# A two-layer decoder kernel: five edits to its mask products, its head norms, its query transposes, its second convolution and its down products

## The chip, the cores and the metric

The kernel runs on one core of one Trainium2 chip. A core has a matrix engine (PE, TensorE; its weight loads are listed as PEld), a vector engine (DVE, VectorE), an activation engine (ACT, ScalarE), a general-purpose engine (POOL, GpSimd) and a queue that issues DMAs (SP, SyncE). PE writes its products to PSUM, which is cut into banks of 128 partitions x 512 float32 values; the other tiles lie in SBUF. Each engine works through its own list of instructions in order and waits at an instruction until what it needs is there.

The metric is the device time of one execution in microseconds (us), and the median over runs is what counts. The time is lower for a better kernel.

## The reference, cut to what matters

The input is `x` (4 sequences, 256 positions, 256 channels) and a context of the same 4 x 256 positions with 128 channels. Two layers follow each other. Each has self-attention, a state-space block that reads the context, and a feed-forward block, each added to `x`.

```
x += L0_attn(layernorm(x))          # 8 query heads of 32, 2 key heads, window of 64 positions
x += L0_mamba(ctx, layernorm(x))
x += L0_ffn(layernorm(x))           # silu(x Wg) * (x Wu), 704 wide, then the down product
x += L1_attn(layernorm(x))          # 16 query heads of 128, 4 key heads, causal
x += L1_mamba(ctx, layernorm(x))
x += L1_moe(layernorm(x))           # 32 experts of 128, weighted by a router, and a shared one
```

In the first attention each head of q, k and v is made zero-mean and divided by its root mean square, and the scores go through a soft cap: `tanh(s / 30) * 30`. Positions outside the window are masked before it.

The state-space block, the same in both layers but for its weights, is

```
xin = ctx @ in_proj.T                         # 256 channels
u   = silu(causal_conv(xin, 4 taps) + bias)   # each channel by itself
dt, Bm, Cm = split(u @ x_proj.T);  dt = softplus(dt @ dt_proj.T + b)
h[t] = h[t-1] * exp(dt[t] * A) + dt[t] * u[t] * Bm[t]     # 16 states per channel
y[t] = sum over states of h[t] * Cm[t];  out = (y + D u) * silu(z)
```

In the second attention the norm of each query head of 128 is followed by a rotation. The norm's root only scales the scores, so it is applied to them and not to the queries.

## The kernel before, in words

Everything is float32 but the mask product. Tokens lie on the partitions in 8 tiles of 128, two per sequence. Time runs in four stages, which overlap at their borders because an engine's list is filled with what is ready.

**The first stage** (`stage_a`, to about 206 us) holds the first attention for the four sequences and most of the first layer's scan. `head0(b)` normalizes a sequence, projects it (L356), rotates it, and takes the head norms: a reduce (L380), the subtraction of the mean (L381), squares (L385), a reduce (L388), and then `rsqrt_steps` (L100 to L112) on 24 columns: one integer guess and three rounds of four short DVE operations, 13 instructions. The result scales the queries (L396), the values (L399) and, on POOL, the keys (L403). `tail0(b)` transposes queries and keys (L424, L429) and computes the scores of two heads at a time in two PSUM banks. The mask is added by a product: `identb` times `far` puts 0 or a large negative number into each bank, and the score products (L453, 32 rows of the array) are added to it. The loop at L447 issues this mask product three times per bank. The first two are overwritten by the third, since each starts its bank anew. Then follow tanh (L462), exp (L470), the products with the values (L476 to L487, 33 columns each), the division (L412, L413), a transpose (L497), and the output product (L506).

Between these, the generator `states` runs the scan: for one state and one half of the channels, ACT takes an exp (L215), POOL multiplies (L217), DVE scans (L218) and multiplies (L220), and the result is added either by a PE product with the identity (L235) or by POOL (L237). The rows for it come by DMA, two per state (L209), issued by SP. The tiles of this chain have three buffers, and the exp's PSUM tile has two.

**The front of the state-space block**, `mamba_front(l, bp, pool)`, serves two sequences `bp` of layer `l`. Input projection and convolution are one step: `conv_taps(l)` (L297) builds on DVE and PE four weight matrices, one per tap (L304, L311, L312). For each half of the channels four products with shifted context (L166) then add up in one bank, and ACT applies bias and silu out of the bank (L173). `conv_taps(1)` is called at L590. The fronts of layer 1 are called at L639, at the end of each half of the feed-forward block, but their convolutions depend on nothing but the context and are done much earlier. The bank is that of the pool `pf`, which has one.

**The feed-forward stage** (to about 310 us) works in two halves of 512 tokens: gates and layer norm, then for each of six blocks of 128 hidden channels the gate and up products (L606), silu (L614) and their product on DVE (L617). Each half ends with the down products: for two token pairs `t2` a bank is taken from the pool `pa`, which has one bank, 12 products are added up in it (L630), and DVE adds the bank to `x` (L638). The pool `pc`, also of one bank, serves gates and layer norms here.

**The second attention** (to about 651 us) walks over 4 sequences x 4 key heads, 16 steps. A step works on three things at once: `queries` of this step, `score` of the step before, `finish` of the one before that. `queries(xnT, g, qT)` (L710) does for both token tiles `c`: `rotate`, a projection into one of two banks (L673), four squares with sums on ACT (L688), and three DVE operations (L693, L700, L701) that leave the rotated queries in `qr`, which has two buffers; then `transposed`, four PE transposes (L707) into one of two banks of the pool `ps_t`, and an ACT copy (L708) into `qT`. At the end comes the root of the norm on POOL (L666). `score` computes the products of one key head (L771, then L780 twice, through one bank of `ps_s` until step 12), which DVE scales and masks (L773, L789), the maxima (L794, L795), the exps (L799) and on POOL the division (L804). `finish` transposes the weights and multiplies them with the values (L814 to L835), and every second step the output product follows (L842). The scan of the second layer runs beside this, 19 of its 32 double steps in the first 13 steps.

**The expert stage** (to the end) is a train of products (L974, L988).

What sets the order: the program's order gives each instruction its rank, but a planner draws up each engine's list when the kernel is built. It plays the program through with estimated durations, and where the next instruction in rank isn't ready it takes a later one that is. So a step of the scan often stands between two steps of a head norm. An instruction that the planner thought ready, and that isn't, holds all that stands behind it on its engine.

Of the kernel before, what the change touches and what calls it, by code (L numbers as in the profile page):

```python
# [41 lines left out]
def decoder_kernel(  # L42
# [34 lines left out]
    def ps(pool):  # L77
        return pool.tile([P, 512], F32, tag="ps", name="ps")
# [71 lines left out]
    def mamba_front(l, bp, pool):  # L150
# [11 lines left out]

        for c in range(2):
            pi = ps(pool)
            for k in range(4):
                mm(  # L166
                    pi.rearrange("p (b t) -> p b t", b=2),
                    lhsT=taps[:, k, c * P : (c + 1) * P],
                    rhs=ctxT[:, 2 * bp : 2 * bp + 2, k : k + S],
                    start=(k == 0),  # L170
                    stop=(k == 3),
                )
            nc.scalar.activation(  # L173
                u[:, c, :], pi, AF.Silu, bias=par[:, o + M_CONVB + c : o + M_CONVB + c + 1]
            )
# [143 lines left out]
    with ExitStack() as ph:  # L319
# [27 lines left out]
        def head0(b):  # L347
# [39 lines left out]
            rs24 = rs.rearrange("p c h -> p (c h)")  # L387
            nc.vector.tensor_reduce(rs24, sq, AX.X, ALU.add)  # L388
            nc.vector.tensor_scalar(rs24, rs24, 1.0 / 32, 1e-6, ALU.mult, ALU.add)
            rs = rsqrt_steps(rs24, 24).rearrange("p (c h) -> p c h", c=2)  # L390
            qn = ap.tile([P, 2, 8, 32], F32, tag="qn", name="qn")
            krep = ap.tile([P, 2, 2, 4, 32], F32, tag="krep", name="krep")

# [25 lines left out]
        def tail0(b, qn, krep, vn, states):  # L419
# [20 lines left out]
            for g in range(2):  # L440
                pr = prs[g]

                for jp in range(2):
                    psc = [ps(pb) for _ in range(2)]


                    for last in range(3):  # L447
                        for p_ in psc:
                            mm(p_[:, 0:320], lhsT=identb, rhs=far, start=True, stop=(last < 2))
                    for klo, qlo, lo, hi in ((0, 0, 0, NEAR), (P, P, NEAR, 320)):  # L450
                        for p_, j in zip(psc, (2 * jp, 2 * jp + 1)):
                            hp = slice(32 * j, 32 * j + 32)
                            mm(  # L453
                                p_[:, lo:hi],
                                lhsT=qkT[hp, 2 + g, klo : klo + P],
                                rhs=qkT[hp, g, qlo : qlo + hi - lo],
                                start=False,
                                stop=(klo > 0),
                            )
                    for p_, j in zip(psc, (2 * jp, 2 * jp + 1)):  # L460
                        for lo, hi in ((0, NEAR), (256, 384)):
                            nc.scalar.activation(  # L462
                                pr[:, j, lo:hi],
                                p_[:, lo and NEAR : (lo and NEAR) + hi - lo],
                                AF.Tanh,
                                scale=256.0 / (math.sqrt(32.0) * SOFTCAP),
                            )
# [109 lines left out]
    with ExitStack() as ph:  # L577
# [9 lines left out]
        nc.sync.dma_start(out=dw, in_=down_in)  # L587
        nc.gpsimd.tensor_mul(dw, dw, downs.unsqueeze(1).to_broadcast([P, NIC, HID]))

        conv_taps(1)  # L590
        scans = []
        for hf in range(2):
            szs = [gates_of(2 * hf + bb, fp, 4) for bb in range(2)]
# [29 lines left out]
                    ALU.mult,  # L623
                )
            for t2 in range(2):
                pd = ps(pa)
                for t in range(2):
                    for ic in range(NIC):
                        m = min(P, INTER - ic * P)
# [14 lines left out]
    with ExitStack() as ph:  # L644
# [62 lines left out]
                nc.tensor.transpose(pt[:, i * P : (i + 1) * P], qr[:, i, :], ident)  # L707
            nc.scalar.copy(dst[:, :, c * P : (c + 1) * P], pt.rearrange("p (h t) -> p h t", h=4))  # L708

        def queries(xnT, g, qT):  # L710

            ss = small.tile([P, 2, 4], F32, tag="qss", name="qss")
            for c in range(2):
                transposed(rotate(xnT, c, g, ss[:, c, :]), c, qT)
            return rsqrt(ss, qks)

        def keys_values(b):
            xnT = work.tile([P, 2, S], F32, tag="xnT", name="xnT")
# [320 lines left out]
        for b in range(B):  # L1039
            xnT, kT = keys_values(b)  # L1040
            for g in range(NKV1):
                qT = ap.tile([P, 4, S], F32, tag="qT", name="qT", bufs=2)
                rq = queries(xnT, g, qT)
                queued.append((b, g, qT, rq, kT, xnT))
                if len(queued) > 1:
                    score()
                if len(scored) > 1:
                    finish()
                step = 4 * b + g
# [137 lines left out]
```

## Time and profile before

| | |
|---|---|
| runs before | 898.40, 910.52 and 914.03 us; median 910.52 |
| the profiled execution | 899.79 us, of which 898.0 us are the span from first to last instruction |
| granted PE clock over the span | 0.947 of full |
| PE busy | 806.3 us, 3074 products |
| DVE busy | 588.0 us |
| ACT busy | 474.5 us |
| POOL busy | 423.5 us |
| chain that ended last | PE 51%, DVE 20%, ACT 10%, issue 5%, POOL 4% |

How to read it: the busy time of an engine is the sum over its instructions. PE's records overlap, so that a stretch of full PE can hold reserves. In the profile, rows cut in slices show how busy an engine was in each part of the span, and the row of the granted clock says at which share of its full speed PE ran. A group of instructions is named by its line in the kernel; after its busy time and mean duration stands how long its engine was idle just before it, and for what. The chain of waits follows the work that ended last back to what released it. Times "from 56 to 206" count from the span's start.

### The profile page before, as it was taken

The page shows a single profiled execution, that of the slowest core. Times are in us where ns is not written, and L with a number is a line of the kernel's source. Part 1 is how long each engine was busy: PE and PEld are TensorE (multiplying, and loading weights), DVE is VectorE, ACT ScalarE, POOL GpSimd, SP SyncE. Part 2 cuts the span into 40 slices and gives each one's busy share as a digit, 9 for nine tenths or more (in the row PEclk, how much of TensorE's full clock was granted, in tenths as well). Part 3 has the DMA queues.
Part 4 walks back from the last instruction along what each step waited for, and adds up shares of the span by engine and source line. Part 5 has one row for each costly group of instructions (what it writes and reads, how often), then busy time and mean ns, then how long its engine had stood idle before and what let it go on. Part 6 is the DMA issues. An engine that isn't in the chain of part 4 may idle for free.

```text
span 898.0 us, 10284 instructions
## 1 busy us (share of the span) xinstructions
PE 806.3 (90%) x3074; PEld 501.4 (56%) x3074; DVE 588.0 (65%) x1106; ACT 474.5 (53%) x1182; POOL 423.5 (47%) x427
## 2 busy tenths in 40 slices
PE   4888999978989887889788978997999999999997
PEld 1445656523444444647555755665666656666665
DVE  4799988985855588797769686787057676212121
ACT  2767544587949556657857754776333433211111
POOL 5456676976645527766547471422257751000000
PEclk9999767978998999999899989997999999999999
DMA  5347564583512401101112010000147753445442
GB/s 162 117 133 252 174 187 157 186 275 100 198 64 68 143 1 36 59 33 39 36 36 72 23 47 1 24 3 24 27 152 226 231 152 104 148 149 162 156 144 82
DMA packets 60999, 98.36 MB, mean 110 GB/s; under 512 B 6336, under 2 KB 26704, under 8 KB 60688
## 3 DMA queue, kind: packets, MB, share of 16 engines
q1 hardware_dynamic: 59232, 95.77, 33.6%
q10 hardware_dynamic: 1712, 1.94, 0.7%
q8 instruction: 24, 0.39, 0.2%
q14 instruction: 31, 0.25, 0.1%
HBM read 96.24 MB, written 1.44 MB: 109 GB/s over the span
## 4 chain that ended last, share of the span: by engine, by line
PE 51%; DVE 20%; ACT 10%; issue 5%; POOL 4%; DMA 1%; DVEq 0%; POOLq 0%; SPq 0%; ACTq 0%
PE ps L974 13%; PE ps L988 12%; PE ps L842 5%; DVE h L218 4%; PE ps L673 3%; DVE hc L220 2%; PE ps L606 2%; PE ps L630 2%; PE ps L827 2%; DVE ps L700 2%; ACT sc L799 2%; DVE qs L693 2%; PE ps L780 1%; ACT L215 1%; PE ps L235 1%
## 5 line engine op out<-in xcount | busy, mean ns | idle before, releaser
L217 POOL TENSOR_TENSOR db<-bt,du 128x512 f32<-128x512 f32 x128 | 162.4, 1280 | 90.7 <-DVE h L218 76.3
L218 DVE TENSOR_TENSOR_SCAN h<-h,db 128x512 f32<-128x512 f32 x128 | 152.9, 1217 | 25.9 <-ACT h L215 25.7
L974 PE MATMUL ps<-moe_xnT,w 128*128 128x512 f32 x272 | 129.0, 597 | 0.0
L988 PE MATMUL ps<-w,hT 128*128 128x256 f32 x544 | 128.7, 380 | 0.0
L979 DVE SCALAR_TENSOR_TENSOR hT<-ps,gr 128x512 f32<-128x512 f32 x64 | 44.1, 689 | 127.0 <-PE ps L974 127.0
L988 PEld LDWEIGHTS ps<-w,hT 128*128 128x128 f32 x544 | 103.2, 191 | 40.2 <-issue 29.4
L215 ACT ACTIVATE h<-dt,negA 128x512 f32<-128x512 f32 x128 | 86.2, 689 | 56.3 <-DVE hc L220 55.7
L980 ACT ACTIVATE hT<-hT 128x512 f32<-128x512 f32 x68 | 42.8, 629 | 133.8 <-DVE hT L979 133.6
L673 PE MATMUL ps<-wqkv,xnT 128*128 128x512 f32 x192 | 93.2, 597 | 8.0 <-DVE rq L665 5.6
L220 DVE TENSOR_TENSOR hc<-h,ct 128x512 f32<-128x512 f32 x128 | 85.1, 680 | 4.0 <-DMA ct<-bc 2.5
L227 POOL TENSOR_TENSOR y<-y,hc 128x512 f32<-128x512 f32 x64 | 80.8, 1274 | 7.1 <-DVE hc L220 7.1
L666 POOL TENSOR_TENSOR rq<-rq,nhalf 128x8 f32<-128x8 f32 x20 | 33.0, 1648 | 88.2 <-DVE rq L665 88.0
L974 PEld LDWEIGHTS ps<-moe_xnT,w 128*128 128x128 f32 x272 | 51.7, 191 | 36.5 <-issue 33.2
L688 ACT ACTIVATE sq<-ps 128x128 f32<-128x128 f32 x160 | 42.4, 282 | 46.2 <-PE ps L673 46.2
L799 ACT ACTIVATE sc<-sc,nm 128x256 f32<-128x256 f32 (+1 forms) x128 | 56.7, 449 | 12.2 <-DVE nm L794 8.0
L804 POOL TENSOR_TENSOR sc<-sc,rsum 128x512 f32<-128x512 f32 (+1 forms) x32 | 46.3, 1468 | 35.2 <-DVE rsum L802 33.6
L842 PE MATMUL ps<-wo,oT 128*128 128x256 f32 x256 | 57.0, 381 | 0.4 <-ACT oT L835 0.4
L842 PEld LDWEIGHTS ps<-wo,oT 128*128 128x128 f32 x256 | 48.1, 190 | 9.2 <-ACT oT L835 2.6
L673 PEld LDWEIGHTS ps<-wqkv,xnT 128*128 128x128 f32 x192 | 32.9, 190 | 29.1 <-issue 17.9
L235 PE MATMUL ps<-hc,ident 128*128 128x512 f32 x64 | 40.6, 723 | 8.1 <-DVE hc L220 8.1
L707 PE MATMUL ps<-ident,qr 128*128 128x128 f32 x160 | 28.7, 297 | 19.2 <-DVE qr L701 17.3
L237 POOL TENSOR_TENSOR y<-y,hc 128x512 f32<-128x512 f32 x32 | 40.8, 1275 | 10.4 <-DVE hc L220 5.3
(201 smaller groups left out, 1447.3 us busy)
## 6 DMA issues: line engine op xcount, KB each, us to landing
bt<-bc SPq DMA_DIRECT2D x96, 256.0 KB, 3.6
ct<-bc SPq DMA_DIRECT2D x96, 256.0 KB, 3.7
w<-in_w_dram SPq DMA_DIRECT2D x64, 256.0 KB, 3.4
gr<-gt SPq DMA_DIRECT2D x64, 256.0 KB, 3.5
wqkv<-in_wqkv_dram SPq DMA_DIRECT2D x1, 3072.0 KB, 14.4
wo<-in_wo_dram SPq DMA_DIRECT2D x1, 2048.0 KB, 8.9
x<-in_x_dram SPq DMA_DIRECT2D x4, 256.0 KB, 5.6
w<-in_ws_dram SPq DMA_DIRECT2D x4, 256.0 KB, 3.4
```

Source lines behind the costliest of these rows:

```text
L215: nc.scalar.activation(h, dt[:, c, :], AF.Exp, scale=negA[:, a : a + 1])
L217: nc.gpsimd.tensor_mul(db, bt, du[:, c, :])
L218: nc.vector.tensor_tensor_scan(h, h, db, 0.0, ALU.mult, ALU.add)
L220: nc.vector.tensor_mul(hc, h, ct)
L227: nc.gpsimd.tensor_add(y[:, c, :], y[:, c, :], state(n, c, bt, ct))
L235: mm(yp, lhsT=ident, rhs=hc, start=(n == 0), stop=(n == 14))
L673: mm(pq, lhsT=xnT[:, f, c * P : (c + 1) * P], rhs=wqkv1[:, f, ch * 512 : (ch + 1) * 512], start=(f == 0), stop=(f == 1),)
L799: nc.scalar.activation(part, part, AF.Exp, bias=nm[:, qc, j : j + 1], accum_out=rsum[:, qc, j : j + 1])
L804: nc.gpsimd.tensor_mul(part, part, rsum[:, qc, :].unsqueeze(2).to_broadcast([P, 4, w]))
L842: mm(pout[:, c * 256 : (c + 1) * 256], lhsT=oTs[h // 4][:, h % 4, c * P : (c + 1) * P], rhs=wo1[:, 8 * gp + h, :], start=(h == 0), stop=(h ...
L974: mm(ph_, lhsT=w[:, f * P : (f + 1) * P], rhs=xnT[:, f, :], start=(f == 0), stop=(f == 1))
L988: mm(po[t // 2][:, (t % 2) * 256 : (t % 2 + 1) * 256], lhsT=h[:, t * P : (t + 1) * P], rhs=w[:, 256:512], start=start and t % 2 == 0, stop ...
```

## The change

1. The mask product of a score bank is issued once, where it was issued three times. There are 32 banks in all, so 64 products of 128 x 320 fall away.
2. The root of the head norms, 24 columns in each of four `head0` calls, is one POOL instruction (a power of -0.5) instead of 13 DVE instructions. The router's `rsqrt_steps` (L945) stays.
3. In a step of the second attention, `queries` now ends after both rotations and the root. The score of the step before comes next, and only then the eight transposes and two copies. `qT` is taken after the score.
4. Layer 1's convolution is done by DVE. One product with the plain projection fills the bank, without shifts, and one DVE multiplication and three multiply-adds on shifted pieces of it give the convolution in SBUF, to which ACT applies bias and silu. `conv_taps(1)` falls away.
5. The two down products of a half take their banks from `pa` and `pc` in turn.

```diff
         for c in range(2):
             pi = ps(pool)
+            if l == 1:
+
+                mm(
+                    pi.rearrange("p (b t) -> p b t", b=2),
+                    lhsT=taps[:, c * P : (c + 1) * P],
+                    rhs=ctxT[:, 2 * bp : 2 * bp + 2, 3 : S + 3],
+                    start=True,
+                    stop=True,
+                )
+                w = par[:, o + M_CONVW + 4 * c : o + M_CONVW + 4 * c + 4]
+                uc = u[:, c, :].rearrange("p (b t) -> p b t", b=2)
+                pt = pi.rearrange("p (b t) -> p b t", b=2)
+                nc.vector.tensor_scalar(uc, pt, w[:, 3:4], None, ALU.mult)
+                for k in range(1, 4):
+                    nc.vector.scalar_tensor_tensor(
+                        uc[:, :, k:S], pt[:, :, 0 : S - k], w[:, 3 - k : 4 - k], uc[:, :, k:S], ALU.mult, ALU.add
+                    )
+                nc.scalar.activation(
+                    u[:, c, :], u[:, c, :], AF.Silu, bias=par[:, o + M_CONVB + c : o + M_CONVB + c + 1]
+                )
+                continue
             for k in range(4):
...
-            rs = rsqrt_steps(rs24, 24).rearrange("p (c h) -> p c h", c=2)
+            nc.gpsimd.tensor_tensor(rs24, rs24, nhalf, ALU.pow)
...
-                    for last in range(3):
-                        for p_ in psc:
-                            mm(p_[:, 0:320], lhsT=identb, rhs=far, start=True, stop=(last < 2))
+                    for p_ in psc:
+                        mm(p_[:, 0:320], lhsT=identb, rhs=far, start=True, stop=False)
...
-        conv_taps(1)
...
-                pd = ps(pa)
+                pd = ps((pa, pc)[t2])
...
-        def queries(xnT, g, qT):
+        def queries(xnT, g):
 
             ss = small.tile([P, 2, 4], F32, tag="qss", name="qss")
-            for c in range(2):
-                transposed(rotate(xnT, c, g, ss[:, c, :]), c, qT)
-            return rsqrt(ss, qks)
+            qrs = [rotate(xnT, c, g, ss[:, c, :]) for c in range(2)]
+            return qrs, rsqrt(ss, qks)
...
+                qrs, rq = queries(xnT, g)
+                if queued:
+                    score()
                 qT = ap.tile([P, 4, S], F32, tag="qT", name="qT", bufs=2)
-                rq = queries(xnT, g, qT)
+                for c in range(2):
+                    transposed(qrs[c], c, qT)
                 queued.append((b, g, qT, rq, kT, xnT))
-                if len(queued) > 1:
-                    score()
```

## The prediction

> **What bounds the kernel now.** I read the page's rows by slice first, then the busy time by stage, then the first stage window by window, then groups, waits and time line where an edit falls.
>
> ```profile
> PE   4888999978989887889788978997999999999997
> DVE  4799988985855588797769686787057676212121
> PEclk9999767978998999999899989997999999999999
> ```
>
> The rows say that PE is the fullest engine everywhere, and that the clock it is granted dips in the first quarter and a little later. By stage (us, then busy time with count of PE, PEld, DVE, ACT, POOL, then clock):
>
> ```profile
> 56.00:206.00 150.00, 136.04 (x585) 81.62 (x584) 130.97 (x202) 87.19 (x165) 107.48 (x100) 0.82 0.61 197
> 206.00:310.00 104.00, 92.03 (x257) 44.06 (x255) 64.95 (x107) 76.82 (x93) 60.20 (x73) 0.95 0.36 117
> 310.00:651.00 341.00, 300.74 (x1265) 199.39 (x1266) 251.60 (x524) 215.89 (x770) 166.31 (x140) 0.96 0.09 30
> 651.00:898.00 247.00, 239.87 (x853) 158.62 (x851) 102.86 (x195) 65.56 (x104) 59.94 (x57) 0.99 0.50 155
> ```
>
> The last stage is a train of products that no edit touches: 247 us stay. The first stage is held by PE and DVE in turn, and the clock decides whose turn it is. Same columns, short windows:
>
> ```profile
> 111.00:114.40 3.40, 3.40 (x29) 2.89 (x28) 3.40 (x8) 1.02 (x2) 2.74 (x4) 1.00 0.19 67
> 121.20:124.60 3.40, 2.73 (x9) 1.32 (x8) 3.40 (x6) 2.35 (x7) 3.38 (x4) 0.50 0.53 127
> 131.40:134.80 3.40, 3.40 (x9) 2.52 (x8) 0.70 (x2) 0.00 (x0) 0.38 (x1) 0.52 0.71 239
> 145.00:148.40 3.40, 3.40 (x10) 1.60 (x8) 3.28 (x5) 1.53 (x3) 3.36 (x4) 0.50 0.51 161
> 158.60:162.00 3.40, 3.40 (x23) 2.02 (x21) 3.40 (x5) 2.67 (x7) 3.40 (x4) 1.00 0.47 154
> ```
>
> At full clock DVE is full. At 0.5 PE takes over, at worst with DVE down to 0.70 of 3.40. Dips follow stretches of small products (29 in one window), about 10 us after each rise: up at 63, down at 74; up at 77, down at 91; up at 94, down at 104; up at 111, down at 121; up at 135, down at 145. From 155 to 192, where sixteen convolution products (L166) run, it stays up.
>
> **Mask products.** 64 of 96 fall away.
>
> ```profile
> L235 PE MATMUL ps<-hc,ident 128*128 128x512 f32 x46 | 31.3, 768 | 8.1 <-DVE hc L220 8.1
> L449 PE MATMUL ps<-far,identb 128*128 128x320 bf16 x79 | 16.8, 349 | 2.9 <-ACT pr L462 2.7
> L166 PE MATMUL ps<-ctxT,taps 128*128 128x512 f32 x26 | 14.6, 678 | 0.5 <-DVE taps L312 0.5
> ```
>
> On the chain from 24 to 190 L449 has 4.0%, 6.6 us; two thirds are 4.4 us gained. Against that stands the clock. The Trainium skill, "TensorE: Matmul & The Clock Gate", section "Why this matters for your kernels", would have the clock fall only after PE-idle gaps of about 3 us. PE's longest wait from 56 to 206 is 2.1 us, so by the rule nothing cools and the edit is worth -4.4. The trace disagrees: the clock is 0.5 in windows where PE records 3.40 of 3.40, so density counts, and these products are the densest work among the scores. Between 121 and 155 seven half-clock windows leave DVE 18.3 of 23.8 us busy: 0.8 us lost in each. Of the 39 windows between 56 and 190 twelve are at half now. If twelve more are, that is 10 us, less 4.4: +6. Bounds: -5 if the clock doesn't care. For the other end I add up PE's need there at the full-clock paces of the chain: 46 L235 at 0.43 are 19.8, 79 L449 at 0.135 are 10.7, 112 L453 at 0.10 are 11.2, 26 L166 at 0.43 are 11.2, 192 value products at 0.11 are 21.1, all others 27: 101 us. The edits take 7.1 (53 mask products), 8.4 (three quarters of L166) and 1.7 (L311). At half clock throughout, 63 doubles to 126, the value products take 0.137 each (26), and PE's waits stay (13.8): 166 against 150, so +17.
>
> **Head norms' root.** Two rows with the same instruction on POOL, 8 and 2 columns:
>
> ```profile
> L666 POOL TENSOR_TENSOR rq<-rq,nhalf 128x8 f32<-128x8 f32 x20 | 33.0, 1648 | 88.2 <-DVE rq L665 88.0
> L126 POOL TENSOR_TENSOR ln_rs<-ln_rs,nhalf 128x2 f32<-128x2 f32 x6 | 4.3, 714 | 0.5
> ```
>
> (1648 - 714) / 6 is 156 ns per column; 24 columns are 714 + 22 x 156 = 4.1 us, an estimate from these rows. "GPSIMD Engine Reference", section "Elementwise — side-by-side cycle accounting", has 2.6 cycles per element for a two-input operation; that would make the root some 0.5 us, 2 us for four, against 16.6 by the rows. The rows are for a power, so I take them. DVE loses 52 short instructions, 19.6 us in the trace (3.3 + 5.4 + 2.1 + 5.4 + 3.4 on L104 and L108 to L111; undisturbed, as at 30.3 to 33.1, 2.8 us per head). What is queued behind: DVE's L396 and L399, with the scan steps the planner put after them, wait for the root; L666's reader L726 waited 3.4 us in all for four such roots, half their length. Half of 4.1 plus half a POOL operation in front (0.6) is 2.7 us per head, 11 us. On POOL, 67% to 75% busy there, four times 4.1 us stand ahead of L217, and DVE's scans wait for that; three buffers of `db` cover two of them, 2.6 us, leaving 1.5 x 4 = 6. So 11 + 6 - 16 (what of 19.6 isn't overlapped records) is about +1, and the first head, uncovered, takes 4.1 for 2.8: +2 in all. Bounds: -12 (all waits covered) to +10 (no cover: 19 + 6 - 16 + 1).
>
> **Query transposes.** Per step eight L707, two copies L708 and two turns of `ps_t` move behind 8 + 8 recorded products of the score, eight scalings on DVE, the exps on ACT and two POOL multiplications. No DMA moves. PE stood 17.3 us for L701 ahead of L707, 14.3 of it in four stalls. One of them:
>
> ```profile
> 438.90 1.12 PE L707 MATMUL ps<-ident,qr 128*128 128x128 f32 x4 [3.21 <-DVE qr L701]
> 440.87 2.08 PE L780 MATMUL ps<-kT,qT 128*128 128x256 f32 x4 [0.85 <-DVE sc L773]
> ```
>
> The product behind the transposes waits for DVE as well, and so it does at 358 (0.46) and 525 (1.31). With the transposes out of the way PE stands as long for L773 and does the transposes later. Only the stall at 611 (4.72) has nothing of the kind: gain 0 to 5. The cost: the two `qr` buffers are freed later, behind products that wait for DVE between banks (0.48 to 1.2 us each), so the next step's L701, and with it the projection banks, may wait. If half a us per step isn't covered, 16 steps cost 8; the cover is that the next L701 comes a projection and three DVE operations later. I take +2, bounds -6 and +12.
>
> **Layer-1 convolution.** Each of four halves: six recorded products fewer, 2.6 us of PE; four DVE operations from PSUM more. The nearest row is L979 (689 ns, same form and size): 2.76 us, 11 us in all. Gone are L304 (1.63), two L312 (1.37) and L311. At 171 to 185 DVE is full: two halves cost 5.5 there, less 3.0: +2.5. The other two (203 to 208 and 256 to 259) find DVE 62% busy and PE on the chain at half clock: -2 to +1. In front of silu 3.44 us become 0.86 + 2.76. The table loads around silu (1.28 us each, 8% of that stage's chain) may fall elsewhere: 2 either way. Together +3, bounds -4 and +8. The lost heat of L166 at 171 to 185 is in the clock sum above.
>
> **Down products.** L638 (0.69) and its signals stand between the two L630 groups in each half: at 303.1 on the chain, 0.65; at 248.8 hidden behind L235. Ten products more can also slip under the silu's table loads. -2, bounds -4 and 0; `pc` is wanted by the second half's gates, which have other work behind them.
>
> **Sum.** 6 + 2 + 2 + 3 - 2 = +11 us: 899.8 becomes 911 for an execution like the profiled one. This lies 10.7 below the median of the runs, so the median of 910.5 becomes 922.
>
> **The rivals.** *Small costs* (52%): the sum above, 908 to 938; 33 of the 52 below the bound of 2% (928.7), which is about what a measurement of this kernel can tell.
>
> *Relief* (20%): DVE is the true bound of the first stage (131 of 150), the clock doesn't react, and DVE gets its 16 us with waits covered. -5 - 8 + 0 + 2 - 2 = -13: 897. For it: full DVE in every full-clock window. Against it: row DMAs (L209) ended waits of 4.8 and 5.6 us on the chain and don't get faster.
>
> *Cold stage* (23%), slower: without the dense products and L166 the clock stays at half from 56 to 206. Need is 63 / c + 24 + 14 us at a clock of c; PE decides from c below 0.56, and at 0.5 the stage costs +17. With +2, +2, +3 and the second half's share the sum is about +24: 934, up to 950. For it: the dips ten us after each rise. Against it: dense work (L235, L506) has always brought it back within 14 us.
>
> *It doesn't happen* (5%): the planner fills the same gaps with the same transposes and only the mask and root edits show: 912.
>
> **Numbers.** Faster: half of relief, 0.11. Slower: the cold stage and 19 of small costs, 0.42. Same: 0.47. The range 889 to 947 leaves out a tenth on each side.
>
> **What would show it.** Clock from 56 to 206 at 0.65 to 0.75; POOL roots of 4.1 us with idle DVE at L396; waits at L707 gone and waits at L780 longer; DVE 8 us fuller around 171 to 260. I am wrong if the clock rises, if roots are short, or if the second attention moves by over 10 us through its order alone.

## The result, and the profile after

| | before | after |
|---|---|---|
| median of runs | 906.38 us (898.40 to 914.03) | 926.34 us (925.70 to 935.24) |
| ratio | | 1.0257, interval [1.0208, 1.0307] |
| profiled span | 898.0 us | 923.9 us |
| last addition to `x` of the feed-forward stage begins | 309.8 us | 333.0 us |
| last addition to `x` of the second attention begins | 651.2 us | 678.1 us |

The changed kernel is slower by 2.6%. The forecast of 922 us lies 4 us from the median, but it was counted from 910.5 us, the median of three runs of the kernel before, and with the fourth run that median is 906.4: forecast was a rise of 11 us, and measured is one of 20 us (medians) to 23 us (ratio). The profiled executions differ by 26 us. Of these, 23 are there at the end of the feed-forward stage, 4 more come in the second attention (341.4 us long before, 345.1 after), and the expert stage gives 1 back. So the first two stages decide.

The rows by slice of the changed kernel, to be held against those of the kernel before:

```profile
PE   4878889965986979889978988996999998999997
DVE  3467877686685759879868974867337676312221
PEclk9888877566995999999999999998999999999999
```

A slice is 23.1 us. From 115 to 231 us the clock has five slices in a row at 7, 7, 5, 6 and 6, and one more at 5 from 277 to 300. The kernel before had 7, 6 and 7 from 90 to 157, one 7 from 180 to 202, and none below 8 in the feed-forward stage after that. The stages of the changed kernel in numbers (us, busy time with count of PE, PEld, DVE, ACT, POOL, then clock, DMA share and GB/s):

```profile
56.00:206.00 150.00, 127.09 (x499) 79.23 (x498) 112.67 (x162) 80.50 (x156) 108.15 (x92) 0.73 0.53 176
206.00:310.00 104.00, 80.67 (x188) 34.35 (x189) 70.16 (x113) 69.59 (x88) 56.62 (x71) 0.78 0.40 120
310.00:651.00 341.00, 299.19 (x1226) 192.03 (x1224) 261.91 (x537) 218.27 (x756) 174.36 (x150) 0.97 0.12 38
651.00:898.00 247.00, 242.41 (x892) 162.55 (x892) 104.29 (x197) 75.25 (x132) 67.59 (x63) 1.00 0.49 150
```

From 56 to 206 the clock went from 0.82 to 0.73, and from 206 to 310 from 0.95 to 0.78. The counts and busy times of PE and DVE are lower too, but the edits themselves took away most of that (the mask products, and of DVE's 19.6 us of steps for the root the 13.8 that came after 56 us). How far the stage had come is better read from the scans: 45 had been begun by 206 us, where the kernel before had begun 49. The third and fourth stage run at 0.97 and 1.00.

Short windows of the changed kernel, 3.4 us each, same columns:

```profile
168.20:171.60 3.40, 3.40 (x16) 3.11 (x15) 0.00 (x0) 1.11 (x3) 3.40 (x4) 0.50 0.52 156
171.60:175.00 3.40, 3.40 (x14) 2.76 (x13) 1.56 (x3) 0.84 (x3) 0.71 (x1) 0.50 0.25 74
175.00:178.40 3.40, 3.40 (x10) 1.53 (x9) 3.36 (x7) 0.24 (x1) 2.98 (x3) 0.50 0.34 118
181.80:185.20 3.40, 3.40 (x18) 3.40 (x18) 1.39 (x2) 0.75 (x2) 3.09 (x7) 0.50 0.59 199
```

The same four windows of the kernel before:

```profile
168.20:171.60 3.40, 2.76 (x16) 1.95 (x15) 2.65 (x4) 2.63 (x7) 3.40 (x4) 1.00 0.66 217
171.60:175.00 3.40, 3.40 (x19) 2.42 (x19) 3.40 (x5) 1.38 (x2) 2.89 (x3) 1.00 0.84 260
175.00:178.40 3.40, 3.40 (x10) 1.44 (x9) 3.40 (x7) 1.10 (x2) 3.17 (x4) 1.00 0.69 255
181.80:185.20 3.40, 3.40 (x11) 1.69 (x9) 2.98 (x4) 3.36 (x6) 3.09 (x6) 1.00 0.84 242
```

In this stretch (171 to 184 us) the kernel before ran 16 of the 32 recorded convolution products of layer 1, at full clock. Now PE is recorded as full and granted one half, and in the first window DVE has nothing to do at all.

The clock is not all of it. From 24 us to the end of the feed-forward stage PE was busy for 254.4 us and idle for 31.4 in the kernel before, and busy for 257.0 and idle for 52.0 in the changed one. So PE, with some hundred products fewer on record, is busy 3 us longer, at a lower clock; the other 21 us are waits of PE, and the lists further down say for what.

The groups of the edits in the changed kernel:

```profile
L256 PE MATMUL ps<-hc,ident 128*128 128x512 f32 x64 | 49.2, 869 | 20.9 <-DVE hc L241 19.4 <-DVE y L260 1.4
...
L724 PE MATMUL ps<-ident,qr 128*128 128x128 f32 x160 | 28.3, 301 | 18.2 <-DVE qr L718 15.0 <-DVE qr L742 2.4
...
L467 PE MATMUL ps<-far,identb 128*128 128x320 bf16 x32 | 9.8, 354 | 2.4 <-ACT qkT L455 1.7 <-ACT pr L480 0.7
...
L167 PE MATMUL ps<-ctxT,inproj 128*128 128x512 f32 x8 | 5.3, 755 | 2.1 <-DVE u L179 1.7 <-ACT dt L211 0.4
```

L467 is the mask product (L449 before), now 32 of it and 9.8 us, for 96 and 19.6 us. L167 is the projection and what is left of the convolution products (L166 before), L256 the addition to the scan's sum (L235 before), L724 the query transposes (L707 before).

The waits by reason, from the list of the changed kernel for all of PE and, in the second fence, for DVE from 0 to 215 us (engine, line, what it waited for: us in total, times, longest):

```profile
PE ps L256 <- DVE hc L241: 19.4, 10, 4.2
PE ps L724 <- DVE qr L718: 15.0, 11, 4.7
PE ps L796 <- DVE sc L789: 2.9, 3, 1.7
```

```profile
DVE qn L417 <- POOL a_rs L411: 16.3, 4, 4.8
DVE rr L387 <- PE ps L377: 13.2, 6, 4.6
```

The additions to the scan's sum now wait 19.4 us for DVE, 8.1 before. The scalings of the heads (L417, before L396) wait 16.3 us for the new root, more than DVE waits for any other thing in this stretch. The transposes wait 15.0 us for the rotated queries, 17.3 before: moving them behind the scores did not take this wait away. A stall of 3.92 us, in the time line of the changed kernel's PE (start, us, line, operation, tiles, and the idle time before it):

```profile
461.74 0.61 PE L787 MATMUL ps<-kT,qT 128*128 128x128 f32 x4
462.18 0.60 PE L724 MATMUL ps<-ident,qr 128*128 128x128 f32 x4
466.70 1.09 PE L724 MATMUL ps<-ident,qr 128*128 128x128 f32 x4 [3.92 <-DVE qr L718]
467.58 0.64 PE L830 MATMUL ps<-ident,sc 128*128 128x128 f32 x2
468.01 1.88 PE L796 MATMUL ps<-kT,qT 128*128 128x256 f32 x4
```

In the program all score products (L787 and L796) now precede the transposes. The planner has put both halves of the transposes (L724) behind L787 and still ahead of L796: L787 of the next step comes only at 472.96. PE waits for the second half's queries, and the score products stand behind it.

### The profile page after: what moved, and what is told of

The parts are those of the page before. It is cut to its first block, busy times and chain, and to the rows that moved or that the text cites. A ratio compares the mean times of both kernels' runs of the same rounds, so it can differ in the third digit from the quotient of the medians.

```text
span 923.9 us, 10063 instructions
## 1 busy us (share of the span) xinstructions
PE 808.6 (88%) x2982; PEld 499.5 (54%) x2982; DVE 580.4 (63%) x1067; ACT 473.9 (51%) x1182; POOL 438.9 (48%) x431
## 4 chain that ended last, share of the span: by engine, by line
PE 41%; DVE 13%; ACT 5%; issue 2%; POOL 2%; DMA 0%; SPq 0%; ACTq 0%; DVEq 0%; POOLq 0%
PE ps L1004 12%; PE ps L990 12%; PE ps L858 5%; PE ps L690 3%; ACT sc L815 2%; DVE h L239 2%; PE ps L796 2%; PE ps L843 2%; DVE qs L710 1%; PE ps L724 1%; DVE ps L717 1%; DVE qr L718 1%; ACT sq L705 1%; DVE sc L805 1%; POOL rq L683 1%
## 5 line engine op out<-in xcount | busy, mean ns | idle before, releaser
L256 PE MATMUL ps<-hc,ident 128*128 128x512 f32 x64 | 49.2, 869 | 20.9 <-DVE hc L241 19.4
L724 PE MATMUL ps<-ident,qr 128*128 128x128 f32 x160 | 28.3, 301 | 18.2 <-DVE qr L718 15.0
```

Source lines behind the costliest of these rows:

```text
L256: mm(yp, lhsT=ident, rhs=hc, start=(n == 0), stop=(n == 14))
```

## The experiments

Three theories stood against each other. *Clock*: what falls away is dense work, TensorE is granted half its speed more often, and the loss follows the granted clock. *Order*: every edit makes the planner draw up other lists, and the new lists are worse. *Work*: the instructions that the edits add (four DVE operations per convolution half, the root on POOL) cost what is lost.

Where a ratio is given, it is against runs of the kernel before on the same chip. "Clock, all runs" is the granted clock over a whole execution, as the median of the runs that the ratio rests on, with the same for the kernel before on that chip behind it. "FFN end" is the start of the last addition to `x` of the feed-forward stage in the profiled execution, "attention" the time from there to the same point of the second attention.

### Each edit alone, on the kernel before

**The mask product once** (`b_mask1`), **the root on POOL** (`b_pow`), **the convolution on VectorE** (`b_conv`), **the transposes behind the scores** (`b_order`) and **two banks** (`b_banks`). The edits are the parts of the diff shown above, for example:

```diff
-                    for last in range(3):
-                        for p_ in psc:
-                            mm(p_[:, 0:320], lhsT=identb, rhs=far, start=True, stop=(last < 2))
+                    for p_ in psc:
+                        mm(p_[:, 0:320], lhsT=identb, rhs=far, start=True, stop=False)
```

```diff
-            rs = rsqrt_steps(rs24, 24).rearrange("p (c h) -> p c h", c=2)
+            nc.gpsimd.tensor_tensor(rs24, rs24, nhalf, ALU.pow)
```

```diff
-                pd = ps(pa)
+                pd = ps((pa, pc)[t2])
```

Expected of the mask edit:

> Kernel before with the mask product issued once, nothing else. Theory 'clock' (the dense products hold the clock up): the granted clock of the first stage (before: 0.82 from 56 to 206 us) falls to 0.72 or less and the kernel takes 6 to 14 us longer, though 64 products are gone. Theory 'root' (the wait for the POOL root is the loss): the clock doesn't matter, 0 to 5 us gained. Theory 'planner' (only the order drawn up changes): anything within 6 us of before, without relation to the clock.

Of the root:

> Kernel before with the head norms' root as one POOL instruction, nothing else. Theory 'root': DVE waits some 16 us for four roots of 4.2 us as in the changed kernel, and the kernel takes 8 to 15 us longer. Theory 'clock': the 52 short DVE instructions that are gone pay for the wait, so 0 to 4 us longer, and what is lost goes through PE standing cold during the wait.

Of the convolution:

> Kernel before with layer 1's convolution on DVE, nothing else. Theory 'clock': the end of the first stage and the feed-forward stage, which had the sixteen products L166 and more, cool (clock from 206 to 310 us from 0.95 to 0.85 or less), 4 to 10 us longer. Theory 'DVE load': 11 us of DVE added and 3 taken, a part of it on the path, +3 us, clock unchanged.

Of the order:

> Kernel before with the query transposes behind the scores, nothing else. From the prediction: +2 us, between -6 and +12, waits of PE at the transposes gone and waits at the second score products longer. Rival: the changed kernel's second attention and expert stage together took only some 3 us longer, so within 3 us of before either way.

Of the banks:

> Kernel before with two banks for the down products, nothing else. From the prediction: -2 us, between -4 and 0, the second group of down products no longer behind the first one's addition. Rival: within noise, since the second half's gates want the bank too: 0 to +2.

Measured:

| kernel | median us | ratio, interval | in us of 907 | forecast | clock, all runs | clock 56-206, 206-310 | FFN end | attention |
|---|---|---|---|---|---|---|---|---|
| mask once | 919.95 | 1.0142 [1.0075, 1.0208] | +12.9 | +6 | .920, .942 | .72, .87 | 322.4 | 348.6 |
| root on POOL | 911.75 | 1.0042 [1.0009, 1.0075] | +3.8 | +2 | .940, .942 | .84, .90 | 322.4 | 341.0 |
| convolution on DVE | 922.74 | 1.0167 [1.0101, 1.0232] | +15.1 | +3 | .915, .942 | .75, .81 | 330.5 | 343.6 |
| transposes later | 907.50 | 1.0004 [0.9976, 1.0031] | +0.4 | +2 | .945, .942 | .79, .89 | 320.5 | 341.5 |
| two banks | 909.17 | 1.0021 [0.9992, 1.0049] | +1.9 | -2 | .940, .940 | .83, .92 | 312.0 | 342.0 |

Two edits carry the loss, the mask product and the convolution, and both come with a lower clock in all their runs. No cost of the transposes can be told from zero, and the banks bring no gain. The sum of the five is 34 us, and the five together cost 20 (medians) to 23 (ratio): the edits overlap in what they lose.

The row of the transposes also says how one profiled execution is to be read. Up to 397 us, well into the second attention, the lists of all four engines in this kernel are those of the kernel before, instruction by instruction. Yet the feed-forward stage ended at 320.5 us instead of 309.8, with the clock at 0.79 and 0.89 instead of 0.82 and 0.95. So 10 us can come and go with the clock from one execution to the next, with nothing changed, and the profiled execution of the kernel before was a lucky one. The runs of the kernel before, 39 on each of three chips, say the same: where the clock of a whole execution is 0.01 lower, the time is 6 to 7.5 us longer (a line fitted to the runs of each chip). I read the FFN ends and the clocks of single executions with that much doubt, and rest the verdicts on ratios and on the clocks of all runs.

The busy and idle time of PE from 24 us to the end of the feed-forward stage tells more of the two edits that carry the loss (profiled executions, us):

| kernel | PE busy | PE idle |
|---|---|---|
| before | 254.4 | 31.4 |
| transposes later (the same lists up to there) | 267.3 | 29.2 |
| mask once | 264.4 | 34.0 |
| root on POOL | 256.5 | 41.9 |
| convolution on DVE | 259.1 | 47.4 |

With the same lists the clock alone moves the busy time by 13 us, so that its size isn't to be read from one execution; the idle time moves by 2. With the mask product once, PE has less work, is busy longer, and waits little more: what is lost there goes with the clock. With the convolution on DVE it waits 16 us more. The row by slice of that kernel shows where, in the slices from 184 to 230 us:

```profile
PE   4888899964995979789988989997999999999997
```

The longest of these waits takes 11.81 us, up to 215.96 us, and is for the normalized input of the feed-forward stage (L140 there, for ACT's L136); in the kernel before PE never waits longer than 2.1 us between 24 and 310 us. ACT waits for POOL (L124 to L127), and POOL, which had first stood 4.33 us, took a multiplication of 3.58 us (L609) before it. In the kernel before the same multiplication (L588) stood behind these norm instructions. That is a change of order among instructions that the edit doesn't touch.

### The same lists, with less of the array at work

To part clock from order I made the two overwritten mask products small without changing anything else: 32 rows and 32 columns of the array instead of 128, for the same 320 columns of data. The number of instructions and their order are those of the kernel before on every engine (`b_slim`).

```diff
-                            mm(p_[:, 0:320], lhsT=identb, rhs=far, start=True, stop=(last < 2))
+                            mm(p_[0 : 128 if last == 2 else 32, 0:320], lhsT=identb[0 : 128 if last == 2 else 32, 0 : 128 if last == 2 else 32], rhs=far[0 : 128 if last == 2 else 32, :], start=True, stop=(last < 2))
```

> Kernel before, but of the three mask products per bank the two that are overwritten use only 32 rows and 32 columns of the array (the third is whole, so the result is the same). Every engine's list has the same instructions in the same order as in the kernel before, so the planner can't be the cause of a difference. Theory 'clock': the dense work is gone, the clock of the first stage falls from 0.8 to 0.72 or less, and 8 to 15 us are lost as with the mask product issued once (+12.8). Theory 'planner': no more than 3 us from before.

Measured: 912.97 us, ratio 1.0065 [1.0036, 1.0095], over 20 runs. The group in this kernel, from what the trace says of that line:

```profile
L449 PE MATMUL ps<-far,identb x96: 291/307/469, 40.2 to 179.5; 32*32 32x320 bf16 x64, 128*128 128x320 bf16 x32
```

The median of 307 ns is close to the 299 of the kernel before: the small products take PE's time just the same. The stages from 56 to 206 and from 206 to 310 of this kernel:

```profile
56.00:206.00 150.00, 142.33 (x569) 81.78 (x569) 122.94 (x190) 79.83 (x157) 100.47 (x93) 0.77 0.53 172
206.00:310.00 104.00, 91.94 (x236) 41.17 (x236) 66.68 (x109) 80.00 (x96) 59.52 (x73) 0.90 0.37 128
```

The clock is 0.77 and 0.90 for 0.82 and 0.95, DVE's busy time there is 122.9 us for 131.0, and the time is 6 us (ratio) to 7 us (medians) longer. That is less than the 8 to 15 us expected of the clock and more than the 3 us at most expected of the order. The two clocks of this one execution would not be enough, since the kernel with the transposes later had 0.79 and 0.89 with the lists unchanged. The runs are: over whole executions the clock has a median of 0.932 in 20 runs (0.927 to 0.944), against 0.940 in the runs of the kernel before on that chip (0.931 to 0.953). At 6.2 us per 0.01, the line through those runs, this goes with 5 us. PE's waits are not the reason: it was idle for 26.1 us from 24 us to the end of the feed-forward stage, for 31.4 before, and busy for 274.1, for 254.4. The order theory leaves no room for a change, since the lists are the same; the work theory neither. Density alone (how much of the array the products use), with nothing reordered, thus costs about half of what the mask edit does.

That the clock falls while PE is full can be seen in four windows of this kernel in a row (same columns as above):

```profile
171.60:175.00 3.40, 3.40 (x21) 1.97 (x21) 2.94 (x5) 2.84 (x7) 1.87 (x3) 1.00 0.18 52
175.00:178.40 3.40, 3.40 (x24) 2.76 (x24) 1.96 (x3) 1.63 (x5) 3.40 (x4) 1.00 0.56 185
178.40:181.80 3.40, 3.40 (x20) 1.94 (x20) 2.97 (x6) 1.21 (x5) 3.37 (x3) 0.86 0.27 84
181.80:185.20 3.40, 3.40 (x15) 2.09 (x13) 3.40 (x5) 2.83 (x6) 2.77 (x3) 0.64 0.87 213
```

PE is recorded as busy throughout, up to 180.5 us mostly with products of 32 rows or of 33 columns, and the clock goes from 1.00 to 0.86 and 0.64.

### More redundant products

If density pays, more of it should pay more. The mask product five times (`b_mask5`) and eight times (`b_mask8`), each overwritten but for the last:

```diff
-                    for last in range(3):
+                    for last in range(5):
...
-                            mm(p_[:, 0:320], lhsT=identb, rhs=far, start=True, stop=(last < 2))
+                            mm(p_[:, 0:320], lhsT=identb, rhs=far, start=True, stop=(last < 4))
```

> Kernel before with the mask product issued five times per bank instead of three, the first four overwritten: 64 products more. Theory 'clock', if there is more to be had: clock from 56 to 206 us above 0.85, 2 to 6 us faster than before. If three products were enough, or PE is the bound: 3 to 9 us slower.

> The kernel before with each mask product issued eight times instead of three (160 products more than the kernel before has in all; the last one starts the sum, so the result is the same). Clock theory: the clock of 56 to 206 us is already .91 with five, so little is left to win; [...] Expected: clock of 56 to 206 us at .92 or more, time 900 to 908 us, within 1% of that with five. Work theory (redundant products cost what they take): 10 us above that with five, 912 us. A time under 898 us would say that the clock had still held back more than the trace's granted clock shows.

Measured: five times 902.22 us, ratio 0.9939 [0.9912, 0.9966] over 20 runs; eight times 920.56 us, ratio 1.0168 [1.0118, 1.0218]. With 64 products more than the kernel before, the kernel is faster by 0.6%: it beats both. The clock over whole executions is 0.955 for 0.937 (median of runs, the kernel before on the same chip behind), and with eight 0.957 for 0.942. The clock row of this kernel, and its first two stages after the start:

```profile
PEclk9996889997999999999999989997999999999999
```

```profile
56.00:206.00 150.00, 128.96 (x640) 82.18 (x640) 138.45 (x211) 84.39 (x164) 108.90 (x100) 0.91 0.61 201
206.00:310.00 104.00, 95.75 (x266) 45.89 (x267) 48.44 (x91) 57.50 (x73) 40.39 (x62) 0.93 0.22 73
```

The clock is 0.91 from 56 to 206, and DVE has done 138.45 us there, 7.5 more than in the kernel before, with 53 scans begun by 206 us for 49. At eight the clock has next to nothing left to win (0.92), and what the products cost remains. The group in both kernels, from 0 to 310 us, first five times, then eight:

```profile
L447 PE MATMUL ps<-far,identb 128*128 128x320 bf16 x160 | 28.1, 316 | 1.9 <-ACT pr L460 1.9
```

```profile
L447 PE MATMUL ps<-far,identb 128*128 128x320 bf16 x256 | 44.6, 319 | 0.9 <-ACT pr L460 0.6
```

The 96 further products are recorded with 16.5 us more. I had allowed 10, which was too low: in the trace these products start 0.14 us apart at full clock and 0.27 at half, so that 96 are 13 us at the least. The miss is larger than that: in the profiled executions the feed-forward stage ends 5.7 us later and the attention is 6.2 us longer, while the medians are 18 us apart. The lists were drawn anew for both, so products and order aren't separated here. The next experiments say something of the attention's share.

### The convolution on VectorE, with the heat given back

The projection of layer 1 is issued four times per half, so that PE does as many dense products as the taps had been; the first three are overwritten.

```diff
+                for _ in range(4):
+                    mm(
+                        pi.rearrange("p (b t) -> p b t", b=2),
+                        lhsT=taps[:, c * P : (c + 1) * P],
+                        rhs=ctxT[:, 2 * bp : 2 * bp + 2, 3 : S + 3],
+                        start=True,
+                        stop=True,
+                    )
```

> Layer 1's convolution on DVE as in the run with that edit alone (+15.6 us), with the projection's product issued four times instead of once; the first three are overwritten. PE has the work of the kernel before again, DVE keeps the 11 us more. Theory 'clock': most of the loss comes back, +2 to +6 us remain, clock from 206 to 310 us above 0.88. Theory 'DVE load' or 'planner': +11 us or more remain.

Measured: 919.85 us, ratio 1.0155 [1.0082, 1.0228], where the convolution alone had 1.0167 [1.0101, 1.0232]. In the total this is no gain, where 2 to 6 us of loss were expected to remain if the clock was the cause. By stage it is one and a loss (the profiled execution, with 914.97 us, is the fastest of the four):

```profile
56.00:206.00 150.00, 133.46 (x546) 81.37 (x545) 124.69 (x190) 77.65 (x153) 97.34 (x89) 0.75 0.54 179
206.00:310.00 104.00, 79.66 (x202) 35.56 (x203) 75.97 (x121) 77.39 (x95) 65.34 (x78) 0.81 0.35 116
```

```profile
56.00:206.00 150.00, 126.62 (x565) 80.51 (x565) 134.46 (x205) 81.08 (x156) 104.73 (x96) 0.81 0.57 191
206.00:310.00 104.00, 92.43 (x253) 43.92 (x254) 56.92 (x99) 54.53 (x72) 42.84 (x61) 0.94 0.25 82
```

The first fence is the convolution alone, the second has the further products. The clock goes from 0.75 and 0.81 to 0.81 and 0.94, and the feed-forward stage ends at 312.4 us instead of 330.5. Over all runs the clock is 0.932 for 0.940, where the convolution alone had 0.915 for 0.942. So giving the missing products back raises the clock. But the attention takes 354.0 us instead of 343.6. The number of scans that DVE had done by the end of the feed-forward stage, in the kernel before (to 310.5 us) and in this one (to 313.1 us), tells what is late:

```profile
L218 DVE TENSOR_TENSOR_SCAN h<-h,db 128x512 f32<-128x512 f32 x72 | 86.6, 1219 | 24.7 <-ACT h L215 24.5
```

```profile
L240 DVE TENSOR_TENSOR_SCAN h<-h,db 128x512 f32<-128x512 f32 x64 | 77.1, 1219 | 10.4 <-ACT h L237 10.3
```

Layer 0 has 64 scans. The kernel before has done 8 of layer 1 as well; here none has begun, and the last copy of the projected context (L202) came only at 313.4 us, where it came at 263.2 in the kernel before. Over all 14 profiled kernels the count is either 72, and then the attention takes 341.0 to 347.2 us, or 64, and then it takes 348.6 to 355.9 (mask once, five times, eight times, and this one). Where it is 64, the feed-forward stage is also relieved of these scans, some 15 us of DVE (8 x 1.22 and as many products with 0.68). So two things are mixed in the 18 us by which that stage ends earlier here: a warmer PE, and less to do. This fits the other half of the mask edit's loss too, with its attention of 348.6 us. It is a pattern over the kernels; no run moved these eight scans alone. A late copy isn't the whole reason either: with the mask product once and five times it came at 288.5 and 272.0 us, and these scans were begun only at 327.2 and 311.2. What is shown for the convolution is that its clock comes back with the products. Its waits don't: PE waits 17.9 us for layer norms (L140, from 24 to 335 us), for 19.3 with the convolution alone and 3.2 in the kernel before. So the 15 us are not the clock's alone, and how they divide between clock and order stays open.

### Parts undone in the changed kernel

The mask product three times again (`a_mask3`), this and the projection four times (`a_heat`), and the 13 DVE steps in place of the root (`a_steps`):

```diff
-            nc.gpsimd.tensor_tensor(rs24, rs24, nhalf, ALU.pow)
+            rs = rsqrt_steps(rs24, 24).rearrange("p (c h) -> p c h", c=2)
```

> Changed kernel with the mask product issued three times again. Theory 'clock': the first stage warms (clock from 56 to 206 us from 0.73 to 0.78 or more) and 5 to 13 us come back, to 913 to 921. If the single edits don't add because the convolution edit alone already keeps the clock down: 0 to 4 us come back.

> Changed kernel with the mask product issued three times again and the layer-1 projection issued four times (the first three overwritten): PE's work of before, with root, order, convolution on DVE and two banks as changed. Theory 'clock': clock from 56 to 310 us from 0.75 to 0.83 or more, 910 to 916. If convolution on DVE and the late front of layer 1 that the convolution with repeated products showed are the loss: 918 or more.

> Changed kernel with the 13 DVE steps for the head norms' root instead of the POOL instruction. In the kernel before the opposite edit cost 4.6 us, so 4 to 6 us come back, 920 to 922, if the edits add. If in the changed kernel the cold clock is what decides and the 16.3 us of DVE waits are covered by it: within 3 us.

| kernel | median us | ratio, interval | clock, all runs | clock 56-206, 206-310 | FFN end | attention |
|---|---|---|---|---|---|---|
| after | 926.34 | 1.0257 [1.0208, 1.0307] | .917, not on record | .73, .78 | 333.0 | 345.1 |
| mask three times | 919.35 | 1.0154 [1.0098, 1.0210] | .933, .940 | .79, .81 | 329.1 | 342.1 |
| and projection four times | 917.63 | 1.0080 [1.0049, 1.0111] | .940, .937 | .83, .85 | 326.7 | 347.2 |
| 13 steps on DVE | 926.91 | 1.0185 [1.0109, 1.0262] | .910, .937 | .68, .77 | 334.8 | 345.2 |

Each dose of redundant products raises the clock and lowers the ratio, from 1.0257 over 1.0154 to 1.0080 (the first two intervals touch, at 1.0208 and 1.0210; the third is clear of the first). That is 16 us of 23 by the ratios (9 us of 20 by the medians, which come from different runs of the kernel before), without taking back any of the work that the edits put on DVE and POOL. The planner drew new lists for these kernels too, so this total is the clock's and the lists' together; that all three values step with the clock is what speaks for the clock. With both given back, the clock of the kernel before is there again (0.940 for 0.937), and 0.8% are still lost; the time lies between the two expectations. These 7 us don't go with a lower clock over the whole execution; PE's idle time up to the end of the feed-forward stage is 42.7 us in that kernel, for 31.4 in the kernel before. With the old steps in place of the root the medians agree within 0.6 us, the ratio is lower by 6.5 us, and the intervals overlap: whether the root costs anything in the changed kernel stays open, where it costs 3.8 us in the kernel before.

## Why the prediction was right, and where it was not

**Direction and size.** 922 was forecast, 926.34 measured, inside the range; the direction is right. That the two lie so close is luck. The rise was forecast at +11 us, a ratio of 1.013, and measured at 1.026 with an interval that begins at 1.021; the too high starting point of 910.5 us made up for 4 us of that. "The same" was given 0.47 and "slower" 0.42, and slower it is. The cold stage, to which I gave 23% and 934 us, was nearer in its mechanism than the "small costs" that I put first: the loss lies in the first two stages, and a good part of it in the clock. It left PE's waits as they were, though, and these are 21 us longer.

**Mask products: right, and low by half.** The sum was +10 for the clock and -4.4 for the work, +6; the edit alone cost 12.9. The part that needs no planner was measured with the same lists at +6 to +7. I had not thought of the planner's part: with the new lists no scan of layer 1 was begun before the feed-forward stage ended. In the changed kernel with its other edits eight were, and giving the products back gained 7 to 9 us. The rule of idle gaps, which the prediction takes from the Trainium skill ("TensorE: Matmul & The Clock Gate", "Why this matters for your kernels"), would have made the edit worth -4.4, and the row of half-clock windows with full PE was the better guide: the clock falls in the windows at 178.4 and 181.8 us shown above with PE busy throughout. The page warns of idle gaps; that nothing else lowers the clock is the prediction's reading of it. The mark set for it, a clock of 0.65 to 0.75 from 56 to 206, was met by 0.73.

The upper bound of +17 has a slip in it: it takes three quarters of 26 L166 away, but 8 of these belong to layer 0 and stay. With 18 the edits take 5.8 us and not 8.4, and the bound is 5 us higher, an estimate from the prediction's own paces.

**Layer-1 convolution: the step that failed.** I had +3 with bounds of -4 and +8, and the edit alone cost 15. I sized it by DVE's work: four operations against those saved. These were sized rightly (L179 took 740 ns, L979 had 689). What was mis-sized is the last sentence of that step, "The lost heat of L166 at 171 to 185 is in the clock sum above": that sum had twelve more half-clock windows up to 190 us, and it had no cold window in the feed-forward stage. The edit alone took the clock of 206 to 310 us to 0.81, where 0.95 and 0.89 were seen in two kernels with the old lists, and that stage ended at 330.5 us for 309.8 and 320.5. The second term that was missing is PE's waits: with that edit alone it was idle 47.4 us up to the end of this stage, for 31.4, and 11.81 us of that are one wait for a layer norm that the new order made late. For this edit the sum had nothing for a new order. How the 15 us divide between the two, the runs don't say. A smaller misreading: of the two later halves only the one at 203 to 208 us had a lowered clock (0.66); at 256 to 259 it was 1.00.

**Head norms' root: right.** 4.1 us were estimated from rows of 8 and 2 columns, and 4.17 measured:

```profile
L411 POOL TENSOR_TENSOR a_rs<-a_rs,nhalf 128x24 f32<-128x24 f32 x4 | 16.7, 4174 | 5.9 <-DVE a_rs L410 5.8
```

The other figure of that step, some 0.5 us, is eight times too low for this instruction: the measurement decides. DVE waited 16.3 us for the four of them, where I had 11; each was nearly uncovered. Alone the edit costs 3.8 us for +2, within the bounds.

**Query transposes: the size held, the reason not.** I said that the waits at the transposes would go and those of the scores grow. Neither came: 15.0 us for 17.3, and 2.9 for 2.6 at the scores. At least in the stall shown, the planner put the transposes ahead of the second score products as before, and PE's wait for the rotated queries stayed. That is the rival "it doesn't happen" for this one edit: nothing won and, with +0.4 us alone, nothing lost.

**Down products: no gain.** -2 was forecast; +1.9 was measured, with an interval from -0.7 to +4.4 us. A gain of 2 us is excluded, a loss isn't shown.

**DVE fuller from 171 to 260: wrong.** It did 61.9 us there instead of 66.8. I had counted the operations of the convolution, and not that a stage that is behind has less of its work in that window.

**The sum.** I added the edits as if each stood alone. Alone they come to 34 us, together to 20 to 23. So the terms were too small by 23 us in all, and that they overlap took back 11 to 14 of it.

## What to carry to other kernels

Before you strike out a product that "does nothing", look whether it lies among small products in a stretch where the granted clock dips: its worth may be the clock of the stage behind it, and a version with the same instruction lists but a smaller tile shows this cheaply. When work moves from the matrix engine to another, price the stage that comes after it at a lower clock, and not only the operations that are exchanged. Split a loss into busy and idle time of the engine in question: here the lower clock made it busy longer, and a new order made it wait. And where a planner draws the lists, count what has been done at a stage's border, since a stage that ends early may have left its work to the next.

## What the runs showed that was not expected

A kernel can be faster with redundant products: five mask products for three gave 0.9939 [0.9912, 0.9966], with the clock at 0.955 for 0.937, and there is a limit, as eight gave 1.0168 [1.0118, 1.0218]. The lists of both were drawn anew, so that the clock's share isn't separated here.

The clock is not the same from one execution to the next where the instructions are. With the same lists on all engines the first two stages ended at 309.8 and 320.5 us. The runs of the kernel before reach from 898.4 to 914.4 us, somewhat wider than this.

The share of the array that is in use counts, and not only whether PE is busy: 64 products of 32 x 32 for 128 x 128, nearly equal in duration, took the clock of whole executions from 0.940 to 0.932 (medians of runs) and cost 0.65% of the time.
